# A search for places moved from a gather loop into the preparation ahead of it, in a two-layer graph network

## The chip, the cores and the metric

The kernel runs on one core of one Trainium2 chip. The metric is the device time of one execution in microseconds (us). Seven executions of the kernel before took 7149.64 to 7173.16 us, with a median of 7166.39 us. The engines are named as in the profile: PE (matrix products), PEld (its weight loads), DVE (vector), ACT (activations and copies), POOL (here above all the issuer of indirect DMAs, that is of gathers) and SP (issuer of plain DMAs).

## The reference

A graph has 12,500 nodes of 128 features and 412,500 edges sorted by destination. Two layers run one after the other:

```python
h = relu(layernorm(x))
msg = where(edge_type == 0, h[src] @ W_data.T + b_data, h[src] @ W_control.T + b_control)
x = x + relu(segment_sum(msg, dst) + h @ W_self.T + b_self)          # layer 0
h = relu(layernorm(x))
g = tanh((h @ gate_w[:128])[dst] + (h @ gate_w[128:])[src] + gate_b)
e = (g + tanh(edge_weight mixed by two scalars)) * 0.5 * d[dst] * d[src]   # d = degree ** -0.5
x = x + segment_sum(h[src] * e, dst)                                  # layer 1
```

The change touches what comes ahead of layer 0's sum over edges, and that sum's loop.

## The kernel before, in words

Nodes are kept in 98 blocks of 128 (NB), edges in tiles of 128. The program is traced as one long sequence, and a scheduler in the framework orders each engine's queue when the kernel is built. It may move an instruction ahead of others that come earlier in the program when it expects it to be ready; instructions marked to be kept in program order (indirect DMAs, the products of the loop) stay in order among themselves. Each engine then runs its queue strictly in order, waiting on semaphores. Pools are opened and closed in a nested way, so that a pool opened later reuses the space of one that was closed, after its last user.

**Preparation.** `nodes()` (L289 to L334) goes over the nodes in 14 batches of 7 blocks. A batch loads x (`xb`), computes means and scales on DVE (L217, L218), the normalised h on ACT (L312), turns h and multiplies it with the three weight matrices on PE (L315, L319), adds the biases on DVE (`y`, L321) and stores two message rows per node in `table1` and the self term in `agg1`. It also keeps h in bf16 parts in `H`. `edges()` goes over the edges in 13 steps: it loads source, destination, type and weight, forms the row of `table1` that each edge needs, turns everything and stores it as `idx1_d` (rows), `dst_d` (destinations) and others, and for later edges stores a flat copy `flat_d`. At its end `windows()` (three steps) finds the lowest and highest destination of each chunk of 28 tiles (`BASE`, `more`) and leaves the lowest destination of each late tile in `tmin`. Two steps of `edges()` follow each batch of nodes.

**The two halves of layer 0's sum.** Edges to the first 56 blocks of nodes (67 chunks of 28 tiles, 1876 tiles in all) are gathered: for each group of 4 tiles (469 groups, `group`, L487), POOL issues four indirect DMAs (L482) that fetch 128 message rows each into one of 8 buffers `M`, DVE builds one-hot matrices `oh` (L493), and PE multiplies and accumulates in `acc` (L258 is the line of the helper `product`). The rows come from `IDX`, the destinations from `DL`: two large tiles in on-chip memory, loaded whole (L461, L462), with `BASE` subtracted from `DL` in one instruction (L464). Edges to the last 42 blocks are not gathered but done densely (`counts`, L698 on): a matrix `A` that counts edges between nodes is built from pairs of codes, `QI` and `CI` (L707 and L709 on DVE, the product `pa` on PE, the copy L712 on ACT), and multiplied with `H` (the product `z`). This is cut into 8264 steps.

**The search.** The codes `QI` and `CI` need to know where each of 2688 pairs of nodes has its edges. `places()`/`sought()` (L511 on) find that: 21 comparisons of all of `tmin` with a bound (`junk`, L537), 21 indirect DMAs for a line of `flat_d` (L547) each followed by a comparison (L550), some arithmetic on 128x21 tiles, 21 indirect DMAs `g` (L577) in 7 blocks of 3, each block followed by some 20 DVE instructions (L589 to L621), and 59 transposes (L648) copied by ACT into `QI`, `CI` and a third array for layer 1. The same generator also zeroes `agg3` (L519 to L523), forms the bounds of a fallback loop, and in 8 steps (L682 to L695) prepares arrays for layer 1.

**The loop of layer 0** (L762 to L796) goes over the groups. After each group it advances the search by two steps; at `lead` = 20 groups the rest of the search is emitted at once, and from then on the dense steps are spread evenly over the remaining groups:

```python
                if not found:
                    found = next(find, True) is True or next(find, True) is True
                    if not found and at < lead:
                        continue
                    if not found:
                        for _ in find:
                            pass
                        found = True
                while done * (groups - lead) < steps * (at - lead):
                    done += 1
                    next(dense, None)
```

At the chunk boundaries the loop loads the rows of `agg1` that the chunk adds to (`old`, L264) and stores the sum (L271), both on SP. After the loop comes a node stage, then layer 1, whose loop gathers in the same way but loads its indices chunk by chunk (`edges_of`, L944, one chunk ahead, three buffers), and a last addition.

Of the kernel before, what the change touches and what calls it, by code (L numbers as in the profile page):

```python
# [18 lines left out]
P = 128  # L19
# [17 lines left out]
def kernel(  # L37
# [235 lines left out]
    with ExitStack() as first:  # L273
# [12 lines left out]
        IDX = pool.tile([P, T1], I32, name="IDX")  # L286
        DL = pool.tile([P, T1], F32, name="DL")
        OK = pool.tile([P, 2], F32, name="OK")

# [89 lines left out]
        def edges():  # L379
            with tc.tile_pool(name="edges", bufs=2) as pool, \  # L380
                    tc.tile_pool(name="edges_t", bufs=2, space=PSUM) as ps_t:
                EC = 2
                for c0 in range(0, NCH, EC):
# [65 lines left out]
                    yield  # L449
            yield from windows()  # L450

        edge_steps = edges()
        for k, _ in enumerate(nodes()):
            for _ in range(2):
                next(edge_steps, None)
        for _ in edge_steps:
            pass

        psum = first.enter_context(tc.tile_pool(name="loop0_p", bufs=1, space=PSUM))
        late0 = first.enter_context(tc.tile_pool(name="late0", bufs=1))  # L460
        nc.sync.dma_start(IDX, idx1_d[:, :T1])  # L461
        nc.sync.dma_start(DL, dst_d[:, :T1])  # L462
        local = DL.rearrange("p (c t) -> p c t", t=C)
        nc.vector.tensor_tensor(local, local, BASE[:, :NC0, None].to_broadcast([P, NC0, C]),  # L464
                                op=ALU.subtract)
        QI = late0.tile([P, NPAIR], F16, name="QI")
        CI = late0.tile([P, NPAIR], F16, name="CI")
# [42 lines left out]
        def places():  # L510
            with tc.tile_pool(name="places", bufs=1) as pool:  # L511
                yield from sought(pool)

        def sought(pool):

            none = pool.tile([P, NBATCH, D], F32, name="none")
            nc.vector.memset(none, 0.0)
            for b0 in range(0, NB, NBATCH):
# [5 lines left out]
            V = pool.tile([P, NJ], F32, name="V")  # L524
            nc.gpsimd.iota(V, pattern=[[2 * P, NJ]], base=N1, channel_multiplier=2,
                           allow_small_or_imprecise_dtypes=True)
            before = pool.tile([P, NJ], F32, name="before")
            inside = pool.tile([P, NJ], F32, name="inside")
            tile_i = pool.tile([P, NJ], I32, name="tile_i")
            rows = pool.tile([P, NJ], I32, name="rows")  # L530
            tile_f = pool.tile([P, NJ], F32, name="tile_f")
            found = pool.tile([P, NJ], F32, name="found")
            found2 = pool.tile([P, NJ2], F32, name="found2")
            first = pool.tile([P, NJ], F32, name="first")
            junk = pool.tile([P, TD], BF16, name="junk")
            for j in range(NJ):
                nc.vector.tensor_scalar(junk, tmin, V[:, j:j + 1], 0.0, op0=ALU.is_lt, op1=ALU.add,  # L537
                                        accum_out=before[:, j:j + 1])
                if j % 4 == 3:
                    yield  # L540
            nc.vector.tensor_scalar(tile_f, before, -1.0, 0.0, op0=ALU.add, op1=ALU.max)
            nc.vector.tensor_scalar(before, tile_f, float(T1 - TF), None, op0=ALU.add)
            nc.vector.tensor_copy(tile_i, before)
            yield
            for j in range(NJ):
                line = pool.tile([P, 8, 3, 16], F32, name="line", bufs=3)
                tc.keep_in_program_order(nc.gpsimd.indirect_dma_start(  # L547
                    out=line.rearrange("p a k e -> p (a k e)"), out_offset=None, in_=flat_d,
                    in_offset=bass.IndirectOffsetOnAxis(ap=tile_i[:, j:j + 1], axis=0)))
                nc.vector.tensor_scalar(junk[:, :P].rearrange("p (a e) -> p a e", e=16),  # L550
                                        line[:, :, 0, :], V[:, j:j + 1], 0.0, op0=ALU.is_lt,
                                        op1=ALU.add, accum_out=inside[:, j:j + 1])
                if j % 3 == 2:
                    yield
            start = pool.tile([P, NJ], F32, name="start")
            nc.vector.scalar_tensor_tensor(start, tile_f, float(P), inside, op0=ALU.mult,
                                           op1=ALU.add)
            nc.vector.tensor_scalar(start, start, 1.0 / 16, None, op0=ALU.mult)
            start = floored(pool, start, [P, NJ], "start")
            nc.vector.tensor_scalar(before, start, float((T1 - TF) * 8), None,  # L560
                                    op0=ALU.add)
            nc.vector.tensor_copy(rows, before)

            nc.vector.tensor_scalar(first, start, 16.0, -float((T2 - T1) * P), op0=ALU.mult,
                                    op1=ALU.add)
            nc.vector.tensor_scalar(start, start, -float(L2 * P // 16), 0.0, op0=ALU.add,
                                    op1=ALU.max)
            nc.vector.tensor_copy(ROWS2, start)
            yield
            q = pool.tile([P, NJ, P], F16, name="q")  # L570
            c = pool.tile([P, NJ, P], F16, name="c")
            c1 = pool.tile([P, NJ2, P], F16, name="c1")
            JB = 3
            for j0 in range(0, NJ, JB):
                g = pool.tile([P, JB, 8, 3, 16], F32, name="g", bufs=2)
                for j in range(JB):
                    tc.keep_in_program_order(nc.gpsimd.indirect_dma_start(  # L577
                        out=g[:, j].rearrange("p a k e -> p (a k e)"), out_offset=None,
                        in_=flat_d.rearrange("t (a e) -> (t a) e", a=8),
                        in_offset=bass.IndirectOffsetOnAxis(ap=rows[:, j0 + j:j0 + j + 1],  # L580
                                                            axis=0)))
                yield
                shape = [P, JB, 8, 16]
                dl, key = g[:, :, :, 0, :], g[:, :, :, 1, :]

                def by16(a):
                    return a.rearrange("p j (a e) -> p j a e", e=16)

                nc.vector.tensor_tensor(dl, dl, V[:, j0:j0 + JB, None, None].to_broadcast(shape),  # L589
                                        op=ALU.subtract)  # L590
                m0 = pool.tile(shape, F32, name="m0")
                m1 = pool.tile(shape, F32, name="m1")
                nc.vector.tensor_scalar(m0, dl, 0.0, None, op0=ALU.is_equal)
                nc.vector.tensor_scalar(m1, dl, 1.0, None, op0=ALU.is_equal)
                nc.vector.tensor_add(m0, m0, m1)
                nc.vector.tensor_reduce(found[:, j0:j0 + JB], m0, AX.XY, ALU.add)
                col = pool.tile(shape, F32, name="col")
                nc.vector.tensor_scalar(col, key, 1.0 / P, None, op0=ALU.mult)
                col = floored(pool, col, shape, "col")
                nc.vector.scalar_tensor_tensor(by16(q[:, j0:j0 + JB, :]), col, -float(P), key,  # L600
                                               op0=ALU.mult, op1=ALU.add)
                cj = by16(c[:, j0:j0 + JB, :])
                nc.vector.scalar_tensor_tensor(cj, m1, float(2 * NB), col, op0=ALU.mult,
                                               op1=ALU.add)
                nc.vector.scalar_tensor_tensor(cj, cj, 1.0, m0, op0=ALU.add, op1=ALU.mult)
                r0 = max(0, J2 - j0)
                if r0 < JB:
                    js2 = slice(j0 + r0 - J2, j0 + JB - J2)
                    ty = pool.tile(shape, F32, name="ty")
                    for r in range(r0, JB):  # L610
                        nc.vector.tensor_scalar(ty[:, r],
                                                iotas[:, :P].rearrange("p (a e) -> p a e", e=16),
                                                first[:, j0 + r:j0 + r + 1], 0.0, op0=ALU.add,
                                                op1=ALU.is_ge)
                    nc.vector.tensor_mul(m0[:, r0:], m0[:, r0:], ty[:, r0:])
                    nc.vector.tensor_reduce(found2[:, js2], m0[:, r0:], AX.XY, ALU.add)
                    nc.vector.tensor_scalar(ty, col, float(NB), None, op0=ALU.is_ge)
                    nc.vector.scalar_tensor_tensor(ty, ty, -float(NB), col, op0=ALU.mult,
# [16 lines left out]
            for k, t in enumerate((T1, T2)):  # L635
                nc.vector.tensor_scalar(OK[:, k:k + 1], pt[:, k:k + 1], float(E - t * P), None,
                                        op0=ALU.is_equal)
# [657 lines left out]
```

## Time and profile before

| | |
|---|---|
| median of 7 executions | 7166.39 us |
| the profiled execution | 7154.53 us, span 7152.8 us |
| first gather of layer 0 issued by POOL | 252.73 us into the span |
| first instruction of the dense half | 504.8 us |
| last product of layer 0's loop ends | 3347.2 us |
| busy over the span | PE 78%, PEld 62%, DVE 67%, ACT 44%, POOL 55% |

The page of the profile lists each engine's busy time, then the span in 40 equal slices (one is 178.8 us) with a digit for the busy tenths of each; PEclk is the tensor clock that was granted. A table by stretches gives, for each stretch, its length and then busy us and (number of instructions) of PE, PEld, DVE, ACT and POOL, then the granted clock, the DMA engines' busy share and GB/s. Groups of instructions are listed as: line, engine, operation, out<-in, shapes, count | busy us, mean ns of one | idle time of the engine just before them, and what ended it. A list of waits says who waited for whom: total us, times, longest us.

### The profile page before, as it was taken

How to read it: one execution, taken by the hardware profiler on the slowest of the kernel's cores; microseconds unless marked ns; L12 is line 12 of the kernel's file. 1: busy time of each engine (PE TensorE's matmuls, PEld its weight loads, DVE VectorE, ACT ScalarE, POOL GpSimd, SP SyncE). 2: the span in 40 equal slices, each digit the busy share in tenths (PEclk: the TensorE clock that was granted, in tenths of full speed). 3: DMA queues.
4: the chain of work that ended last, by engine and by line, in shares of the span. 5: the costliest groups of instructions: out<-in, count | busy, mean ns of one | idle time of the engine just before them, and what ended most of it. 6: DMA issues, size and time to landing. Idle time of an engine off the chain costs nothing. (4 is left out here: it accounts for less than half of the span.)

```text
span 7152.8 us, 106835 instructions
## 1 busy us (share of the span) xinstructions
PE 5601.4 (78%) x33125; PEld 4413.8 (62%) x33126; DVE 4807.2 (67%) x16203; ACT 3179.1 (44%) x9128; POOL 3926.6 (55%) x4152
## 2 busy tenths in 40 slices
PE   5338898898889888886288785887888888888884
PEld 3226676676666666665033233787887878878774
DVE  6556665666666666666777776776777777777775
ACT  6214444444444444443322223555555555555551
POOL 2465665565566556552255555555555555555552
PEclk7659999999999999998589997898989988888897
DMA  6421121121122112113544552111111111111115
GB/s 193 138 83 46 47 49 44 46 49 45 45 48 49 45 47 49 45 46 87 154 129 136 134 135 76 46 47 44 48 46 47 47 46 46 46 46 46 47 47 144
DMA packets 455853, 493.50 MB, mean 69 GB/s; under 512 B 131482, under 2 KB 352238, under 8 KB 455282
## 3 DMA queue, kind: packets, MB, share of 16 engines
q0 software_dynamic: 131360, 274.09, 15.8%
q1 hardware_dynamic: 272672, 185.32, 9.2%
q10 hardware_dynamic: 51250, 27.19, 1.4%
q8 instruction: 271, 4.44, 0.2%
q14 instruction: 300, 2.46, 0.1%
HBM read 411.55 MB, written 74.70 MB: 68 GB/s over the span
## 5 line engine op out<-in xcount | busy, mean ns | idle before, releaser
L899 POOL DMA_INDIRECT M<-table,ix x2128 | 2018.9, 949 | 1509.4 <-issue 749.5
L482 POOL DMA_INDIRECT M<-table,IDX x1876 | 1787.5, 953 | 1179.1 <-issue 448.8
L258 PE MATMUL z<-H,A 128*128 128x385 bf16 x8232 | 1901.4, 333 | 24.3 <-PE pa L258 14.5
L712 ACT CAST A<-pa 128x392 bf16<-128x392 f32 x2688 | 1270.8, 487 | 1340.2 <-PE z L258 629.8
L258 PEld LDWEIGHTS <-A 128*128 128x128 bf16 x8232 | 1130.2, 138 | 767.4 <-issue 480.3
L707 DVE TENSOR_SCALAR oq<-piota,QI 128x128 bf16<-128x128 f16 x2688 | 748.9, 279 | 892.4 <-PE z L258 428.1
L258 PE MATMUL acc<-M,oh 128*128 128x128 f32 (+1 forms) x8008 | 1182.2, 292 | 176.0 <-DMA M<-table,IDX 117.5
L258 PEld LDWEIGHTS acc<-M,oh 128*128 128x128 f32 x8008 | 1089.4, 204 | 335.6 <-issue 130.8
L258 PE MATMUL z<-A,HS 128*128 128x128 f32 x6664 | 1030.9, 293 | 166.5 <-issue 144.4
L258 PE MATMUL pa<-oc,oq 128*128 128x392 bf16 x2688 | 894.0, 333 | 319.7 <-issue 223.0
L709 DVE TENSOR_SCALAR oc<-piota,CI 128x392 bf16<-128x392 f16 x2688 | 1111.8, 414 | 0.0
L258 PEld LDWEIGHTS z<-A,HS 128*128 128x128 f32 x6664 | 953.2, 205 | 199.0 <-issue 176.8
L258 PE MATMUL pa<-oc,oe 128*128 128x196 f32 x4352 | 937.0, 361 | 154.6 <-ACT oe L1084 71.0
L1094 ACT COPY A<-pa 128x392 f32<-128x392 f32 x1088 | 500.3, 484 | 1045.4 <-PE pa L258 444.1
L258 PEld LDWEIGHTS pa<-oc,oe 128*128 128x128 f32 x4352 | 793.9, 209 | 199.7 <-ACT oe L1084 86.1
L912 ACT ACTIVATE gate<-e,M 128x1 f32<-128x1 f32 x2128 | 511.4, 292 | 629.9 <-DVE only L905 280.8
L905 DVE SCALAR_TENSOR_TENSOR only<-piota,dl,pd 128x128 f32<-128x128 f32 x2128 | 738.5, 347 | 61.6 <-remote 25.3
L920 DVE TENSOR_SCALAR oh<-piota,dl,e 128x128 f32<-128x128 f32 x2128 | 725.6, 404 | 0.1
L1084 ACT ACTIVATE oe<-oq,eb 128x128 f32<-128x128 f32 x2176 | 683.4, 393 | 45.4 <-DVE oh L920 13.4
L1079 DVE TENSOR_TENSOR oc<-piota,cb 128x784 f32<-128x784 f32 x544 | 526.0, 967 | 44.4 <-remote 14.8
L1076 DVE TENSOR_TENSOR oq<-piota,qb 128x512 f32<-128x512 f32 x544 | 371.7, 683 | 100.0 <-ACT oe L1084 100.0
L258 PE MATMUL ev<-ms,which 98*8 98x512 f32 x552 | 308.5, 643 | 81.1 <-DVE ms L998 65.2
(262 smaller groups left out, 3349.1 us busy)
## 6 DMA issues: line engine op xcount, KB each, us to landing
qs<-src_q SPq DMA_DIRECT2D x138, 256.0 KB
bs<-src_b SPq DMA_DIRECT2D x138, 256.0 KB
M<-table,ix POOLq DMA_INDIRECT x2128
M<-table,IDX POOLq DMA_INDIRECT x1876
table<-y SPq DMA_DIRECT2D x14, 903.0 KB
xb<-in_x_dram SPq DMA_DIRECT2D x26, 448.0 KB
agg<-y ACTq DMA_DIRECT2D x14, 451.5 KB
ga<-agg SPq DMA_DIRECT2D x14, 451.5 KB
```

The source lines that it names most:

```text
L258: tc.keep_in_program_order(nc.tensor.matmul(*args, **how))
L482: tc.keep_in_program_order(nc.gpsimd.indirect_dma_start(out=M[:, s, :], out_offset=None, in_=table1, in_offset=bass.IndirectOffsetOnAxis(a ...
L707: nc.vector.tensor_scalar(oq, iota_q, QI[:, k:k + 1], None, op0=ALU.is_equal)
L709: nc.vector.tensor_scalar(oc, iota_c, CI[:, k:k + 1], None, op0=ALU.is_equal)
L712: nc.scalar.copy(A[:, i], pa)
L899: tc.keep_in_program_order(nc.gpsimd.indirect_dma_start(out=M[:, s, :], out_offset=None, in_=table2, in_offset=bass.IndirectOffsetOnAxis(a ...
L905: nc.vector.scalar_tensor_tensor(only, iota_1, dl[:, s:s + 1], pd, op0=ALU.is_equal, op1=ALU.mult, accum_out=e[:, s:s + 1])
L912: nc.scalar.activation(gate[:, s:s + 1], e[:, s:s + 1], AF.Tanh, bias=M[:, s, D:])
L920: nc.vector.tensor_scalar(oh[:, s, :], iota_1, dl[:, s:s + 1], e[:, s:s + 1], op0=ALU.is_equal, op1=ALU.mult)
L1079: nc.vector.tensor_tensor(oc, iota_c[:, None, :].to_broadcast([P, 4, NC1]), cb[:, us, None].to_broadcast([P, 4, NC1]), op=ALU.is_equal)
L1084: nc.scalar.activation(oe[:, k, :], oq[:, k, :], AF.Copy, scale=eb[:, 4 * u + k:4 * u + k + 1])
L1094: nc.scalar.copy(A[:, 4 * u + k:4 * u + k + 2, :], pa)
```

## The change

The search becomes part of a generator `searched()` that runs `edges()`, `windows()` and `places()` one after another; four of its steps, in place of two, follow each batch of nodes, and whatever is left is emitted after the thirteenth of the 14 batches. The transposes of the codes are issued block by block inside the search, into two PSUM buffers; the scaling by `OK`, which the copies after the transposes did, becomes two DVE instructions over the whole of `CI` and `C1`. The buffers `line` and `g` have one copy less each. What the generator did beside the search (zeroing `agg3`, bounds, the arrays for layer 1) stays in the loop as `afterwards()`, one step per group. `lead` goes, and the dense steps are spread over all 469 groups. `IDX` and `DL` go: each chunk's `ix` and `dl` (14 KB each) are loaded two chunks ahead into three buffers, and DVE subtracts `BASE` for each.

The diff, cut to its core:

```diff
-        IDX = pool.tile([P, T1], I32, name="IDX")
-        DL = pool.tile([P, T1], F32, name="DL")
         OK = pool.tile([P, 2], F32, name="OK")
+        QI = pool.tile([P, NPAIR], F16, name="QI")
+        CI = pool.tile([P, NPAIR], F16, name="CI")
...
-            yield from windows()
-
-        edge_steps = edges()
-        for k, _ in enumerate(nodes()):
-            for _ in range(2):
-                next(edge_steps, None)
-        for _ in edge_steps:
-            pass
-
-        nc.sync.dma_start(IDX, idx1_d[:, :T1])
-        nc.sync.dma_start(DL, dst_d[:, :T1])
-        local = DL.rearrange("p (c t) -> p c t", t=C)
-        nc.vector.tensor_tensor(local, local, BASE[:, :NC0, None].to_broadcast([P, NC0, C]),
-                                op=ALU.subtract)
...
         def places():
-            with tc.tile_pool(name="places", bufs=1) as pool:
-                yield from sought(pool)
+            with tc.tile_pool(name="places", bufs=1) as pool, \
+                    tc.tile_pool(name="places_p", bufs=1, space=PSUM) as psum:
+                yield from sought(pool, psum)
...
-                line = pool.tile([P, 8, 3, 16], F32, name="line", bufs=3)
+                line = pool.tile([P, 8, 3, 16], F32, name="line", bufs=2)
...
-            q = pool.tile([P, NJ, P], F16, name="q")
-            c = pool.tile([P, NJ, P], F16, name="c")
-            c1 = pool.tile([P, NJ2, P], F16, name="c1")
+            C1 = pool.tile([P, NJ2 * P], F16, name="C1")
+            identh = pool.tile([P, P], F16, name="identh")
+            nc.vector.tensor_copy(identh, ident)
+
+            def turned(a, to, j0):
+                w = a.shape[1]
+                pt = psum.tile([P, 512], F32, name="misc", bufs=2).bitcast(F16)
+                for j in range(w):
+                    nc.tensor.transpose(pt[:, j * P:(j + 1) * P], a[:, j, :], identh)
+                nc.scalar.copy(to[:, j0 * P:(j0 + w) * P], pt[:, :w * P])
+
             JB = 3
             for j0 in range(0, NJ, JB):
-                g = pool.tile([P, JB, 8, 3, 16], F32, name="g", bufs=2)
+                g = pool.tile([P, JB, 8, 3, 16], F32, name="g", bufs=1)
...
+                turned(q, QI, j0)
...
+                turned(c, CI, j0)
...
+                    turned(c1, C1, j0 + r0 - J2)
...
+            nc.vector.tensor_scalar(CI, CI, OK[:, 0:1], None, op0=ALU.mult)
+            nc.vector.tensor_scalar(C1, C1, OK[:, 1:2], None, op0=ALU.mult)
+            nc.sync.dma_start(qi_d, QI)
+            nc.sync.dma_start(ci_d, C1)
             yield
-            for a, to, held_to in ((q, QI, qi_d), (c, CI, None), (c1, None, ci_d)):
...
+        def searched():
+            yield from edges()
+            yield from windows()
+            yield from places()
+
+        search = searched()
+        for k, _ in enumerate(nodes()):
+            for _ in range(4):
+                next(search, None)
+            if k == NB // NBATCH - 2:
+                for _ in search:
+                    pass
...
-        find = places()
+        find = afterwards()
         dense = counts()
-        found = False
         groups = T1 // S
-        lead = 20
         steps = PPH + NHB * NB
         done = 0
+        def edges_of(c):
+            ix = pool.tile([P, C], I32, name="ix", bufs=3)
+            nc.sync.dma_start(ix, idx1_d[:, c * C:(c + 1) * C])
+            dl = pool.tile([P, C], F32, name="dl", bufs=3)
+            nc.sync.dma_start(dl, dst_d[:, c * C:(c + 1) * C])
+            nc.vector.tensor_scalar(dl, dl, BASE[:, c:c + 1], None, op0=ALU.subtract)
+            return ix, dl
+
         last = old = None
+        ready = {c: edges_of(c) for c in range(2)}
         for c in range(NC0):
+            if c + 2 < NC0:
+                ready[c + 2] = edges_of(c + 2)
+            ix, dl = ready.pop(c)
             acc = psum.tile([P, D + 1], F32, name="acc", bufs=2)
             for g in range(0, C, S):
                 t = c * C + g
-                group(acc, IDX[:, t:t + S], DL[:, t:t + S], t, g == 0, g + S >= C)
+                group(acc, ix[:, g:g + S], dl[:, g:g + S], t, g == 0, g + S >= C)
...
-                if not found:
-                    found = next(find, True) is True or next(find, True) is True
-                    if not found and at < lead:
-                        continue
-                    if not found:
-                        for _ in find:
-                            pass
-                        found = True
-                while done * (groups - lead) < steps * (at - lead):
+                while done * groups < steps * at:
                     done += 1
                     next(dense, None)
+                next(find, None)
```

## The prediction

> **What bounds the kernel now.** I read the 40 slices of the page first. They show layer 0's loop full on PE from the fourth slice on, and a hole ahead of it.
>
> ```profile
> span 7152.8 us, 106835 instructions
> ...
> PE   5338898898889888886288785887888888888884
> ...
> PEclk7659999999999999998589997898989988888897
> ```
>
> The reader is to see the 3 in slices 2 and 3 of PE, and granted clocks of 0.6 and 0.5 there, between a preparation at 5 and a loop at 8 or 9. A table by stretches then cuts the hole open. Its limits are those of the stages: first gather at 252.73 us, comparisons of the search until 304, its first DMAs until 359, its blocks until 443, transposes until 505, the dense half until 3347.
>
> ```profile
> 0.00:150.00 150.00, 82.36 (x263) 45.98 (x264) 102.05 (x339) 87.51 (x199) 35.94 (x61) 0.80 0.74 206
> 150.00:252.00 102.00, 63.24 (x190) 33.92 (x190) 58.48 (x162) 58.85 (x140) 26.73 (x27) 0.83 0.46 131
> 252.00:304.00 52.00, 11.43 (x32) 7.80 (x32) 39.64 (x64) 0.00 (x0) 15.97 (x17) 0.50 0.55 159
> 304.00:359.00 55.00, 12.37 (x32) 8.01 (x32) 20.24 (x90) 0.00 (x0) 35.53 (x37) 0.50 0.42 122
> 359.00:443.00 84.00, 23.39 (x66) 15.50 (x67) 64.22 (x173) 3.14 (x7) 66.41 (x58) 0.50 0.39 113
> 443.00:505.00 62.00, 16.66 (x100) 15.09 (x99) 6.69 (x34) 8.27 (x9) 42.30 (x45) 0.53 0.26 70
> 505.00:3347.00 2842.00, 2500.69 (x15428) 1917.06 (x15428) 1803.43 (x5972) 1327.77 (x3023) 1668.13 (x1764) 0.97 0.19 46
> ```
>
> In the 253 us from 252 to 505 PE is busy for 64 us at half clock, in the 2842 us after it for 88%. In the same 253 us only 168 records of `acc` products stand, 8 for a group, so 21 groups of 469. Who sets the pace of the dense stage is told by the waits from 600 to 3300 us:
>
> ```profile
> POOL M L482 <- issue: 402.9, 1314, 0.6
> DVE oq L707 <- PE pa L258: 349.8, 269, 4.6
> POOL M L482 <- PE z L258: 309.0, 212, 6.0
> POOL M L482 <- PE pa L258: 221.5, 136, 7.6
> ```
>
> POOL, DVE and ACT wait for PE. The rate agrees: 632 `acc` records in each 500 us are 79 groups, 6.33 us a group, where POOL needs 4 x (0.95 + 0.30) = 5.0 us for its four gathers. So PE sets the end of this stage, and the 253 us before it are a wait for the search: the dense half cannot start without `QI` and `CI`.
>
> **The change, part by part.** Times are against the profiled execution (7154.53 us, 11.86 us under the median); the difference is then put on the median.
>
> *The hole goes.* Dense work no longer waits for 20 groups of gathers and the search. That takes away 505.4 - 252.7 = 252.7 us, and gives back three things.
>
> *The 21 groups* now run inside the dense stage. At the end of the loop, at full clock, a group's eight records start at 3304.78 and the next product at 3305.67: 0.89 us. 21 x 0.89 = 19 us. Their DVE and POOL parts lie beside PE: POOL's 5.0 us against a new pace of (2842 + 19) / 469 = 6.10 us.
>
> *The start of the dense half.* The first product needs four gathers (5.0 us) and a landing, some 3 us: 8 us behind the first gather. What stays in `afterwards()` (8 steps of some 2.6 us for layer 1's arrays, 6 us of bounds) falls on ten groups in which DVE is at 63% already: 26 us into some 60 us with 22 free. I give 8 us for it and for the 6.4 MB of zeroes beside the first gathers; both stood in the hole before. Nothing to 20 us.
>
> *The preparation grows.* This is the large unknown. DVE is the busiest engine there: 102.05 + 58.48 = 160.5 us, less `DL` and four `oh` that go or were the loop's, 155 us. The search's own DVE time: the four stretches from 252 to 505 hold 39.6 + 20.2 + 64.2 + 6.7 = 131 us, of which about 40 belong to `oh` (18 x 0.69), layer 1's arrays (20), bounds and the rest. That leaves 91 us. The two multiplications by `OK` are not in the trace; nearest is L709, 414 ns for 392 columns, so 2688 and 2176 columns are at most 5.1 us, at least nothing (no gain: the copies they relieve are ACT's). Sum 155 + 91 + 5 = 251 us.
>
> ```profile
> L537 DVE TENSOR_SCALAR_CACHE_REDUCE junk<-tmin,V 128x1347 bf16<-128x1347 f32 x21 | 33.9, 1614 | 5.1 <-POOL V L525 4.9
> L577 POOL DMA_INDIRECT g<-flat_d,rows x21 | 20.8, 991 | 10.8 <-issue 5.5 <-DVE start_f L566 4.7 <-DMA M<-table,IDX 0.6
> ```
>
> The other engines have room: POOL 63 us and 42 x 1.25 = 52 more; ACT 146, with 20 copies of 384 columns in place of nine of up to 896; PE 146, with the same 59 transposes. The bounds for the first gather: below, DVE never idle but for its first 8 us and the landing of the last table, 251 + 16 = 267 us. Above, the search simply put behind the old preparation: comparisons 45.5 us, 21 lines at 1.25 us and landings 32, to the first `g` 3, seven blocks 82, the end 5, together 168, so 421 us. That lower bound has reasons to fail: each comparison after a gather waits in DVE's queue for its landing, with the batch's arithmetic behind it; one buffer of `g` puts a block's three gathers behind the reads of the one before; POOL's subtractions for `H` and the search's gathers block each other in order. DVE's best long stretch in this very work, 359 to 443, was 76% busy. I take that: 251 / 0.76 = 330 us. So +77 us.
>
> *Indices by chunk.* `IDX` and `DL` go (issued at 112 and 123 us, hidden); 134 loads of 14 KB come, on SP. SP has idle time but waits in order: it stood 888 us for `o` of the dense half (longest 36.2) and 354 for `R` (longest 52.0). Behind a blocked load stand `old` and the next stores; POOL would wait for `ix`. The loads are two chunks (some 85 us) ahead, POOL runs at most 8 groups (49 us) ahead of PE; the margin is about 36 us less one landing. Layer 1 does the same one chunk ahead; POOL's idle time there names no load of `ix`:
>
> ```profile
>   issue: 749.5, 1726
>   ACT A L1094: 359.7, 156
>   ACT gate L912: 185.1, 69
> ```
>
> 67 subtractions at 236 ns (layer 1's L1148) are 16 us of DVE beside PE, with over 1000 us free. So I cost it at nothing. Uncovered, it costs a landing per chunk: the weights issued at 15.02 us were used at 18.26, 3.2 us x 67 = 214 us.
>
> [...]
>
> *Sum.* First gather 330, + 8 + 2842 + 19 + 8 = 3207 us in place of 3347: -140 us. Layer 1 is untouched. 7154.5 - 140 = 7014.5 for the profiled execution, 7166.4 - 140 = **7026 us** against the median.
>
> **Rivals.**
> *The search hides wholly in DVE's idle time* (92 of 252 us idle speaks for it, the waits in order against): first gather 267, -203 us, 6963.
> *The search is merely put behind the nodes*: for it, the chain of landings, one buffer of `g` and POOL in order; against it, the steps alternate with batches, which have idle DVE. First gather 421, -49 us, 7117. This is also the case where the move does not do what it says.
> *The loop is paced by groups, not by PE*: then 21 groups cost 21 x 6.33 = 133, not 19; -26 us, 7140. Against it: POOL waits for PE.
> *Slower: the chunk loads come late on SP*, held behind a store that waits for ACT's `o`, as the 36.2 and 52.0 us above allow. It decides from 140 / 67 = 2.1 us a chunk; at 3.2 us it is 214 - 140 = +74 us, 7240.
>
> **How the numbers follow.** Forecast 0.58, hidden wholly 0.18, put behind 0.12, paced by groups 0.05, late loads 0.07. The range goes from 6970 (near the full hiding) to 7120 (just past the search put behind), and leaves out the last two cases and the edges of the others, 0.2. A measurement here tells some 0.2% (14 us) from no change. Slower by more: 0.06 of the late loads. Within: 0.03, from the last two. Faster: 0.91.
>
> **What would show it.** The first gather at 300 to 370 us with DVE about 76% busy before it; the first `pa` about 8 us later; then 2860 to 2880 us to the end of the loop, 6.1 us a group, POOL still waiting for PE and not for `ix`; layer 1's length as before. I am wrong if the first gather comes after 421, if POOL or DVE wait for DMAs of `ix` or `dl`, or if the dense stage is longer than 2900 us.

## The result, and the profile after

The changed kernel takes 7210.29 us (median of 17 executions, 7195.93 to 7242.81), the kernel before beside it 7166.46 us (42 executions): a ratio of 1.0068, 95% interval [1.0057, 1.0078]. It is slower by 0.7% where 2% faster was forecast. The same kernel later gave 1.0008 [0.9984, 1.0032] beside other executions of the kernel before, so its cost lies between nothing and 0.7%; no run shows the forecast gain. The profiled execution took 7229.64 us, with a span of 7227.8 us.

Executions fell on chips of two speeds. The median of the kernel before is 7158 to 7188 us on some (three chips, "the slower chips" below) and 5791 to 5793 us on others (two, "the faster chips"). In the experiments a ratio is always to the kernel before on the same chip. The kernel after itself ran on slower chips alone.

The slices of the page answer to those of before:

```profile
span 7227.8 us, 107419 instructions
...
PE   5378888888888888887188885888888888878884
...
PEclk7689999999999999998589897998998899988897
```

Of the hole's two digits 3 on PE, one is left. But the loop behind it, which the forecast took for full, has no 9 where before had three, and it fills more of the 19th slice (7 in place of 6), not less. The stretches, cut at the first gather and the first dense product (us, then busy us and number of PE, PEld, DVE, ACT and POOL, granted clock, DMA share, GB/s):

```profile
0.00:314.00 314.00, 161.74 (x485) 84.26 (x486) 225.74 (x674) 148.40 (x348) 98.36 (x124) 0.72 0.58 161
314.00:375.00 61.00, 6.26 (x35) 4.09 (x36) 30.52 (x77) 6.02 (x13) 37.83 (x38) 0.50 0.31 95
375.00:3400.00 3025.00, 2583.93 (x15579) 1957.91 (x15578) 1861.90 (x6146) 1331.01 (x3020) 1739.80 (x1844) 0.95 0.20 49
```

The dense half starts at 375.4 us in place of 505.4, 130 us earlier. Its stage then lasts 3025 us in place of 2838: 187 us more, for 20 more groups. The loop's last gathered product is at 3395.1 us in place of 3338.1, +57; the other 18 us of the span's +75 lie behind the loop, where nothing was changed. (The 2838 us end with the last `z`, at 3343.8; the 2842 us of the prediction, and the 3347.2 us of the table ahead of it, run on to the closing products of the dense half.) In the stage PE is busy for 2583.93 of 3025 us: 441 us idle, where before had 340:

```profile
505.00:3343.00 2838.00, 2498.08 (x15415) 1915.64 (x15415) 1802.87 (x5971) 1327.20 (x3020) 1668.13 (x1764) 0.97 0.19 46
```

Who waits in that stage (600 to 3300 us; total us, times, longest us):

```profile
ACT A L712 <- PE z L258: 669.0, 583, 3.3
PEld L258 <- issue: 555.0, 782, 4.3
...
PE pa L258 <- issue: 274.6, 311, 4.1
...
DVE dl L772 <- DMA dl<-dst_d: 1.7, 2, 1.4
```

The last line clears the chunk loads: 1.7 us in all. The first three look like a circle: ACT waits for PE, and PE's weight loads and `pa` wait for nothing that the profile shows ("issue"; 467.0 and 218.4 us before). The timeline shows one turn of it (start us, us, engine, line, operation, and the idle time before with its releaser):

```profile
1507.26 1.05 PE L258 MATMUL acc<-M,oh 128*128 128x129 f32 x8
...
1509.14 0.66 PE L258 MATMUL z<-H,A 128*128 128x385 bf16 x3
...
1509.69 0.94 POOL L620 DMA_INDIRECT M<-table,ix  x1 [0.59 <-PE pa L258]
1510.20 0.49 ACT L712 CAST A<-pa 128x392 bf16<-128x392 f32 x1 [2.59 <-PE z L258]
1510.21 0.28 DVE L707 TENSOR_SCALAR oq<-piota,QI 128x128 bf16<-128x128 f16 x1 [2.14 <-PE z L258]
...
1510.74 0.33 PE L258 MATMUL pa<-oc,oq 128*128 128x392 bf16 x1 [0.94 <-issue]
```

The reader is to see the order. A group's eight gathered products stand at 1507.26. Some 2 us behind them POOL, ACT and DVE, idle until then, are released within 0.5 us of each other, all three by PE, though the `pa` that ACT copies ended 1.6 us before by its record (the line of 1508.31, 0.33 us long, is left out here). PE then stands 0.94 us because ACT and DVE were late. Such gaps of PE (over 0.4 us) come to 0.90 us a group, 0.71 before.

The trace also holds the times at which semaphores rise, and POOL, ACT and DVE wait here for one that PE raises at the ends of its products. In the kernel before, in the 252 us ahead of its first gather, it rises 0.01 us behind the end of each of the 266 products that raise it. In this turn of the kernel after it rises at 1510.18, 1.5 us behind the recorded end of `pa`, and ACT starts 0.02 us later. From 600 to 3300 us the next rise comes 0.21 us behind the end of such a product at the median, over 1.0 us behind one in ten, and 3.9 us behind at most. 881 times two rises stand 35 to 50 ns apart, where the recorded ends of two products that raise it are never less than 0.16 us apart. There it is PE's signals that are late, not its products.

### The profile page after: what moved, and what is told of

Read it like the earlier page. It is cut to its first block, busy times and chain, and to the rows that moved or that the text cites. A ratio compares the mean times of both kernels' runs of the same rounds, so it can differ in the third digit from the quotient of the medians.

```text
span 7227.8 us, 107419 instructions
## 1 busy us (share of the span) xinstructions
PE 5646.8 (78%) x33125; PEld 4411.4 (61%) x33126; DVE 4832.3 (67%) x16271; ACT 3175.5 (44%) x9135; POOL 3903.7 (54%) x4152
## 5 line engine op out<-in xcount | busy, mean ns | idle before, releaser
L902 POOL DMA_INDIRECT M<-table,ix x2128 | 2011.1, 945 | 1533.7 <-issue 742.3
L620 POOL DMA_INDIRECT M<-table,ix x1876 | 1772.0, 945 | 1276.5 <-issue 452.1
L258 PE MATMUL z<-H,A 128*128 128x385 bf16 x8232 | 1931.7, 337 | 28.1 <-PE pa L258 18.6
L1001 DVE SCALAR_TENSOR_TENSOR ms<-bs,pidx,gp 98x512 f32<-98x512 f16 x276 | 203.3, 745 | 254.3 <-PE gp L258 74.8
```

Of the source, the lines that this page charges most:

```text
L258: tc.keep_in_program_order(nc.tensor.matmul(*args, **how))
L620: tc.keep_in_program_order(nc.gpsimd.indirect_dma_start(out=M[:, s, :], out_offset=None, in_=table1, in_offset=bass.IndirectOffsetOnAxis(a ...
L902: tc.keep_in_program_order(nc.gpsimd.indirect_dma_start(out=M[:, s, :], out_offset=None, in_=table2, in_offset=bass.IndirectOffsetOnAxis(a ...
```

## Experiments

The first account was: the dense stage has become dearer. Either *by its loads* (indices by chunk, on SP and DVE), or *by its groups* (each costs some 6 us there, whatever stands beside it, and the hole had hidden 20 of them).

**Indices whole again, and the dense half's place.** `e1_whole_idx` is the kernel after with `IDX` and `DL` whole and `afterwards()` emitted ahead of the loop:

```diff
+        nc.sync.dma_start(IDX, idx1_d[:, :T1])
+        nc.sync.dma_start(DL, dst_d[:, :T1])
...
-            ix, dl = ready.pop(c)
+            ix, dl = IDX[:, c * C:(c + 1) * C], DL[:, c * C:(c + 1) * C]
```

> The changed kernel with IDX and DL loaded whole again, ahead of the loop, and with everything of afterwards() emitted ahead of the loop (the two large tiles leave no room for it beside the dense half), which starts the dense half some 30 us later. Theory C, the chunk loads: each of the 67 chunk boundaries stalls the loop by some 2 us, through DVE's subtraction or SP; then the dense stage, 3027 us in the changed kernel, falls to 2860 to 2890 us, and the time to about 7100 us. Theory S, the spreading: the dense stage grows because 469 groups, not 448, interrupt it and because 17.6 steps in place of 18.4 fall between two groups, which leaves PE at half clock more often; then the stage stays at 3000 to 3030 us and the time is about 7230 us.

`e2_chunks` is the kernel before with the loads by chunk (the opposite edit):

> The kernel before with one part of the change: ix and dl loaded by chunk, two chunks ahead, in place of IDX and DL. Theory C: the dense stage grows from 2842 us to about 2970, the time from 7166 to about 7295 us. Theory S: the dense stage stays within 20 us of 2842, the time within 20 us of 7166.

`e3_lead` is the kernel after with the dense half held back for 20 groups, as before:

```diff
-                while done * groups < steps * at:
+                while done * (groups - 20) < steps * (at - 20):
```

> The changed kernel with the dense steps spread over the last 449 groups again, as before the change; the first 20 groups run alone, at POOL's 5 us a group, beside the end of the search. Theory S: the dense stage is 2842 us within 20 and starts at about 420 us, so it ends near 3262, and the time is about 7075 us. Theory C: the stage is about 2970 us and the time about 7200 us.

`e4_whole_lead` has both edits, with `afterwards()` left in the loop:

> Both undone: IDX and DL whole, dense steps over the last 449 groups; what is left of the change is the search in the preparation. Both theories: dense stage 2842 us within 20, start at about 420 us, time about 7075 us. If the stage is longer than 2900 us, both are wrong, and something that the move itself does to the order of the queues is the cause.

Measured: e1 1.0040 [1.0016, 1.0064], e2 0.9974 [0.9951, 0.9998], e3 0.9936 [0.9894, 0.9978], e4 0.9968 [0.9946, 0.9990]. The loads are no cost: alone they change the time by -0.3%, and taken out of the changed kernel they leave its long stage (e1: 3057 us). The stage's length goes with the number of groups in it: 2838 to 2906 us where it has 448 (before, e2, e3, e4), 3025 to 3057 us where it has 468 (after, e1). Theory C falls with e1 and e2. Theory S's own numbers for e3 and e4 (7075 us) were missed: they took 7135 and 7155 us, since the dense half started at 502 and 495 us and not at 420, and the stages were over 50 us longer than 2842. Holding the dense half back for 20 groups, that is giving most of the gained start away again, made the kernel no slower.

**What the gathers cost, part by part.** `e5_dense_only` leaves the gathered half out, `e6_no_gather` leaves only the 1876 indirect DMAs out (`held` is a buffer of constants, given to every group of layer 0):

```diff
-            M = pool.tile([P, S, D + 1], F32, name="M", bufs=MB)
-            for s in range(w):
-                gather(M, s, ix[:, s:s + 1])
+            if held is None:
+                M = pool.tile([P, S, D + 1], F32, name="M", bufs=MB)
+                for s in range(w):
+                    gather(M, s, ix[:, s:s + 1])
+            else:
+                M = held
```

> The changed kernel with the gather half of layer 0's loop left out (no gathers, one-hots, products, loads and stores of its 469 groups): what the 8264 dense steps cost by themselves. If a group costs what PE's records show (0.89 us), the stage is some 2884 - 469 x 0.89 = 2470 us at full clock. If the loop is paced by its groups, each of which costs 5 us or so, it is far shorter, about 1900 us, near the sum of the dense records (8232 x 0.165 + 2688 x 0.165 + 84 x 2.3 = 1995 us).

> The changed kernel with the 1876 indirect DMAs left out: the products of every group run as they did, on one buffer of constants. If it is the gathers (POOL's pace, their traffic) that make a group dear, the stage falls to the dense one alone plus 469 x 0.89 = 417 us. If it is the products on PE, or the interruption of the chain PE, ACT, DVE by them, it stays near 3025 us, or 2884 us less half-clock time.

`e7_spread_400` is the kernel after with the dense steps spread over the first 400 groups only, so that 20.7 of them stand beside a group in place of 17.7:

```diff
-                while done * groups < steps * at:
+                while done < steps and done * 400 < steps * at:
```

> The changed kernel with the dense steps spread over the first 400 groups, 20.7 steps a group, and the last 69 groups by themselves at POOL's 5 us. Theory S in its strict form (a group in the dense stage costs 5 us or more, whatever steps stand beside it): the dense half ends after some 400 x 6.2 = 2480 us at full clock, 2600 with half-clock time, and 69 x 5 = 345 us follow, so that the time is some 80 us below the changed kernel's. If a group costs 0.89 us, the dense half takes 2884 - 69 x 0.89 = 2823 us and the 345 us come on top: some 280 us above it.

`e8_before_again` is the kernel before, for a profile of the same chip:

> The kernel before, profiled a second time on the chip of these runs. All theories: the dense stage is 2842 us long within 30. How far it and its half-clock time (151 us in the first profile) differ tells how much of the differences between the stages of two profiles is chance.

These four fell on a faster chip, where the kernel before takes 5790.93 us. They gave 5288.7 us (e5), 5721.63 (e6), 5986.67 (e7, 1.0338 [1.0321, 1.0355]) and 5793.47 (e8). There the dense stage is what the forecast took it for. The stretch of the dense stage in e8, the kernel before:

```profile
465.00:2840.00 2375.00, 2369.58 (x15416) 1889.04 (x15416) 1832.24 (x5969) 1371.89 (x3020) 1690.09 (x1787) 1.00 0.26 56
```

PE is busy for 2369.58 of 2375 us, at a clock of 1.00. And there a tighter spread costs 3.4%: it lengthens the tail of gathers at the end of the loop (310 us in e7), in which PE has little to do (197 us busy). Whether the move pays on such a chip was not run; an estimate from e7's start of the dense half (372.7 us) and e6's stage (2412 us) ends it at 2785 us, 55 us before e8's.

So the same kernels were run on a slower chip, with the kernel after beside them:

> The changed kernel without the gather half of layer 0's loop, again, since the last four kernels ran on a chip on which the kernel before takes 5791 us and its dense stage stands without gaps. On a chip where it takes 7166 us: if the gaps in front of pa come with the groups' products, they vanish here and the stage is near 1995 us; if the chain of PE, ACT and DVE stalls by itself on such a chip, the stage is 2300 us or more.

> The changed kernel without the 1876 indirect DMAs, again. On a chip where the kernel before takes 7166 us: if the gathers cause the gaps, the stage is 2412 us as on the other chip; if the products do, it stays near 3025 us.

> The changed kernel with the dense steps over the first 400 groups, again. On a chip where the kernel before takes 7166 us and 1.0 to 1.4 us is lost in each group of the dense stage: the dense half ends after 2348 + 416 x 1.2 = 2850 us, the last groups add 5 us each, 260 us, and the time is some 60 us above the changed kernel's. If the loss belongs to steps, not groups, the dense half takes 2900 us or more.

> The changed kernel beside the kernel before, on the chip of these runs. Where the kernel before takes 5791 us (dense stage 2375 us, no gaps) the working of the prediction should hold: dense start near 375 instead of 465 us, stage 2375 + 18 us, so 70 us faster, 5720 us. Where it takes 7166 us, 40 to 50 us slower, with a stage near 3025 us.

Measured: f5 6092.27 us, f6 6509.69, f7 6965.61 (0.9749 [0.9722, 0.9776]), f9 7164.16 (1.0008 [0.9984, 1.0032]). Between f5 and f6 lie 417 us for 469 groups of products: 0.89 us a group, the very term of the prediction. The stage of f6, with all products and no indirect DMA:

```profile
364.00:2775.00 2411.00, 2396.71 (x15577) 1906.31 (x15575) 1865.56 (x6145) 1372.63 (x3020) 0.00 (x0) 0.99 0.04 10
```

2411 us for 468 groups, 5.15 a group, PE full: this is what PE needs, on the slower chips as on the faster (2412 in e6). The same products behind gathers take 3025 us. So the gathers cost the stage 614 us, and f7 says that the cost shrinks when more dense steps stand beside each group: on the slower chips the tighter spread that loses 3.4% on the faster gains 2.5%. That was not expected: f7 was forecast some 60 us above the kernel after, and f9 itself 40 to 50 us above the kernel before.

**Issue or transfer, floor or price, move or spread.** `g1_spread_430` is f7 with 430 in place of 400:

> The kernel after with the dense steps spread over the first 430 groups (19.2 steps a group in place of 17.6); 39 groups of gathers are left behind for PE to do without dense work. Theory G (a group beside dense work costs about 6.2 us whatever number of steps stands beside it): the stage of dense work has some 440 groups and lasts about 440 x 6.2 = 2730 us, the rest of the gathers adds some 39 x 5 = 195 us, and the loop ends near 3310, between the kernel after (3395) and the spread over 400 (3223). Rival P (PE paces the stage: 8264 steps cost the same, spread as they like): the stage is as long as the kernel after's, 3027, less only 0.89 us for each of the 28 groups it is rid of, and the tail is added: slower than the kernel after by some 100 us.

`g2_before_spread` puts the same spread on the kernel before:

```diff
-                while done * (groups - lead) < steps * (at - lead):
+                while done < steps and done * (400 - lead) < steps * (at - lead):
```

> The kernel BEFORE (search still in layer 0's loop) with the dense steps spread over groups 21 to 400 in place of 21 to 469. It tells whether the gain of the spread over 400 (ratio 0.975 on the kernel after) is the spread's alone or needs the move. Theory M (where PE is kept full, the move pays what was forecast): it is slower than the kernel after with the same spread, by 252.7 us of hole less 77 us of longer preparation less 19 us for 21 groups and some 35 us of late start: some 100 to 120 us. Rival S (the move gives nothing in any spread, since its 21 groups cost what the hole cost): both take the same time within 30 us.

`g4_spread_400` is f7 once more, beside it:

> The kernel after with the dense steps spread over the first 400 groups, once more, beside the same spread on the kernel before. Expected as the last time: loop's end near 3223, ratio about 0.975 to the kernel before. Theory M has it some 100 to 120 us faster than the kernel before with the same spread, rival S within 30 us of it.

`g3_plain_loads` keeps the transfers and takes them from POOL (`plain` is set in layer 0's loop):

```diff
-                gather(M, s, ix[:, s:s + 1])
+                if plain:
+                    r = (t + s) * P
+                    nc.sync.dma_start(M[:, s, :], table1[r % (NB * P):r % (NB * P) + P, :])
+                else:
+                    gather(M, s, ix[:, s:s + 1])
```

> The kernel after with each of layer 0's 1876 gathers replaced by a plain load of 128 consecutive rows of the same table into the same buffer, issued by SP; the sums of layer 0 over the gathered edges are therefore those of other rows. Same products, same bytes, same number of transfers; POOL issues no indirect DMA in this loop. Theory D (the gathers' making on POOL, their descriptors, is what delays PE's signals and costs half clock): stage near that without gathers, 2411 us for 468 groups, without gaps. Rival B (the transfers themselves, bytes into memory beside PE, cost the gaps): stage near the kernel after's, 3027 to 3036 us, with gaps of some 1.1 us a group.

Measured: g1 7100.52 us, 0.9897 [0.9861, 0.9934]; g2 6966.63, 0.9713 [0.9677, 0.9748]; g4 6986.06, 0.9738 [0.9701, 0.9775]; g3 6520.13. The stage of g3:

```profile
363.00:2775.00 2412.00, 2393.77 (x15578) 1902.40 (x15577) 1866.23 (x6145) 1369.84 (x3020) 0.00 (x0) 1.00 0.26 61
```

As many bytes land in the same buffers (DMA share 0.26, more than the 0.20 of the kernel after), and the stage is as short as without any. In f6 and g3 PE's semaphore rises 0.01 us behind the end of a product, 99 times in 100. So it is not the amount of traffic that makes 2412 us into 3025, but that POOL issues it as indirect DMAs; the rival that blames the bytes falls. One difference g3 leaves: its rows are consecutive, those of the gathers scattered. Against it stands that the gathers land as soon on both kinds of chips (the last packet of one comes 1.22 us behind the end of POOL's instruction in the kernel after, 1.28 us in e7; medians, packets taken in order).

The profiled runs of layer 0 with groups on the slower chips, by the dense steps beside one group (rounded down to whole us). "PE's need" is f6's 2411 us less 0.89 us for each group that the stage lacks. It is good to some 20 us: for the 448 groups of the kernel before it gives 2393 us, and e8 took 2375. Half clock is the time in the stage at half the tensor clock, at which eight gathered products took 2.06 us (at 373.58 us in the kernel after), for 1.05 us at full (at 1507.26 us); the last column is the stage less half of that time, for each group.

| kernel | steps a group | groups | stage, us | PE's need | excess | half clock, us | us a group |
|---|---|---|---|---|---|---|---|
| after, f9, e1 | 17.7 | 468 | 3025, 3036, 3057 | 2411 | 614 to 646 | 287, 280, 341 | 6.16 to 6.19 |
| before, e2, e3, e4 | 18.4 | 448 | 2838, 2893, 2906, 2896 | 2393 | 445 to 513 | 151, 235, 245, 214 | 6.17 to 6.23 |
| g1 | 19.3 | 429 | 2777 | 2376 | 401 | 184 | 6.26 |
| g4, f7 | 20.7 | 399 | 2499, 2480 | 2350 | 149, 130 | 65, 37 | 6.18, 6.17 |
| g2 | 21.8 | 379 | 2350 | 2332 | 18 | 26 | 6.17 |
| f6, g3 (no indirect DMA) | 17.7 | 468 | 2411, 2412 | 2411 | 0, 1 | 29, 21 | 5.12, 5.13 |

With four gathers, every row gives 6.2 to 6.3 us a group, whatever number of steps stands beside it. At 21.8 steps PE's own need is 2332 / 379 = 6.15 us a group, as long as that pace, and the excess is nearly gone. So in these runs on the slower chips a group of four gathers has a floor of about 6.2 us beside dense work (6.16 to 6.26 in the table); PE's need shows only above it. A price on each gather does not fit: at 614 / 468 = 1.31 us a group, 523 us would be left in g4, where 149 were measured. Rival P of g1, in which PE paces the stage, falls. Theory G holds, though the stage of g1 has 429 groups and not the 440 of its forecast, and the loop ended at 3350 us, not 3310.

And the move? g2, without it, is no slower than g4, with it (6966.63 and 6986.06 us, overlapping intervals); theory M asked for 100 to 120 us between them. The stretches from the first dense product to its end and of the tail, g2 first, then g4:

```profile
505.00:2855.00 2350.00, 2326.18 (x14866) 1825.03 (x14866) 1773.24 (x5892) 1341.35 (x3020) 1428.95 (x1515) 0.99 0.22 48
2855.00:3210.00 355.00, 119.66 (x551) 101.06 (x550) 46.09 (x76) 0.16 (x1) 233.93 (x248) 0.57 0.23 50
```

```profile
384.00:2883.00 2499.00, 2389.37 (x15024) 1846.42 (x15023) 1802.46 (x6060) 1338.73 (x3020) 1510.65 (x1596) 0.99 0.24 52
2883.00:3241.00 358.00, 119.47 (x555) 102.17 (x554) 47.34 (x83) 0.16 (x1) 234.57 (x248) 0.57 0.23 50
```

The dense half starts 121 us earlier in g4 and lasts 149 us longer: 20 groups at the pace of the table are 123 us, half of the added half-clock time is 20. Both beat both kernels of this study, by the spread alone.

The tails speak of the same thing. With no dense work beside them, the last 69 groups take 358 us in g4, 5.2 us each, while PE works for 119 us and POOL for 235. On the faster chip the same tail takes 310 us (e7), which is what 248 gathers every 1.25 us need. Three lines of g4's tail (lines of POOL and SP between them left out):

```profile
2993.05 2.09 PE L258 MATMUL acc<-M,oh 128*128 128x129 f32 x8 [5.85 <-issue]
...
3007.69 0.69 DVE L631 TENSOR_TENSOR oh<-piota,dl 128x512 f32<-128x512 f32 x1 [14.70 <-remote]
...
3008.43 2.09 PE L258 MATMUL acc<-M,oh 128*128 128x129 f32 x8 [13.30 <-issue]
```

PE's products end at 2995.1 by the records; DVE's next `oh` comes 12.5 us later, having waited 14.70 us for something that the profile can't name ("remote"), while POOL issued a gather every 1.25 us throughout. The record of the semaphores can: `oh` waits for the one that PE raises. Behind these products it rose at 2995.76, 2997.87 and 3007.66, and DVE started 0.02 us after the last of these. At 3020.27, with POOL idle since 3015.0, it rose ten times in 0.38 us, where eight products took 2.09 us: signals that had been held back, not products that ended then. In e7's tail every rise stands 0.01 us behind the end of its product. PE goes on 0.05 us after DVE's end. It is the way from PE's products to those who wait for them that is late, not the way back.

**Two that told little.** Two last kernels were to split the cause further. `g6_half_plain` replaces every second gather by a plain load, `g5_unread` lets the gathers run and the products read a constant buffer:

> The kernel after with every second gather of layer 0 replaced by a plain load of 128 consecutive rows, issued by SP (so half of the gathered edges get other rows). Theory F (a floor: a group of four gathers by POOL takes some 6.1 us, and PE's own need of 5.15 us shows only above it): with two gathers the floor is near 3.1 us, the stage is PE's own, about 2411 us, without gaps. Rival A (each indirect DMA adds its price, 614 us / 1872 = 0.33 us): half of it stays, about 2720 us.

> The kernel after with its gathers issued and landing as before, but layer 0's products over the gathered edges read a constant buffer, so PE does not wait for a landing and POOL does not wait for PE; those sums are therefore of constants. Theory I (issuing alone delays the signals by which PE releases ACT and DVE): gaps of 0.5 us a group or more remain, the stage of 468 groups lasts 2700 us or more. Rival W (the cost needs the wait of POOL for PE and of PE for the gather): no gaps, stage near that without gathers, 2411 us, POOL done early.

Both fell on a faster chip (kernel before 5792.7 us), which has no excess to split: g6's stage of 2412 us (5726.05 in all) is PE's need, but full gathers leave it there too. g5 took 7051.05 us, for another reason. From 600 to 2700 us (the second line is from the list of SP's own queue):

```profile
DVE dl L774 <- DMA dl<-dst_d: 1197.6, 23, 72.2
```

```profile
SPq L771 <- DMA M<-table,ix: 1831.7, 147, 34.5
```

With POOL free to run ahead, SP's load of the next `ix` waits for the gathers that still read its buffer (1831.7 us), the load of `dl` stands behind it on SP, DVE waits for that in order (1197.6 us), and PE waits for DVE (`pa` for `oc`, 1125.1 us). That is a late load, as in the prediction's slower rival, but held by the gathers' reads of `ix` and not by a store. In the kernel after it does not happen (1.7 us of waits); there POOL runs at most the 8 buffers `M` ahead.

## Why the prediction was wrong

**The step that failed** is "*The 21 groups* now run inside the dense stage ... 21 x 0.89 = 19 us", with its ground, "So PE sets the end of this stage". The 0.89 us are right (f5 against f6), and on the faster chips PE does set the end (busy for 2369.58 of 2375 us in e8). On the slower chips the 20 groups cost 187 us: about 123 by the pace (20 x 6.16) and 68 by half the added half-clock time, (287 - 151) / 2. The stage passed the 2900 us that the prediction gave as a sign of being wrong. Of the 198 us by which the dense half's closing products ended later than forecast (3405 us for 3207), 161 are this stage and 37 its later start. The kernel before already ran at this pace, 445 us above PE's need, and so the hole was not idle time to be won: its 21 groups went through there beside the search, at no cost to the dense stage. The trace had shown it. PE was busy for 2500.69 of 2842 us at a clock of 0.97, so 341 us were missing, and the waits from 600 to 3300 us held a line that I passed over:

```profile
PEld L258 <- issue: 467.0, 669, 4.0
```

That POOL waits for PE did not say here that PE is busy; PE's word came late (in this stretch 0.27 us behind the end of a product at the median, over 1.0 us behind one in ten).

**The start of the dense half**, forecast 8 us behind the first gather, came 61 us behind it. The first gather at 314.6 us (forecast 330) was near, but for another reason than given: it waits (5.23 us) for the last store of `table1` by the nodes, not for the end of the search. The search's last lines stand here:

```profile
356.79 0.56 DVE L531 TENSOR_TENSOR g<-g,V 128x384 f32<-128x384 f32 x1 [12.33 <-DMA g<-flat_d,rows]
...
371.15 0.78 DVE L587 TENSOR_SCALAR C<-C,OK 128x2176 f16<-128x2176 f16 x1
...
373.58 2.06 PE L258 MATMUL acc<-M,oh 128*128 128x129 f32 x8 [3.57 <-DVE oh L631]
```

The last block's `g` stood in POOL's queue behind the first gathers of the loop; DVE waited 12.33 us for its landing, and the loop's `oh` and products stand in order behind the block's arithmetic. The dense half began 37 us later than forecast (375.4 for 338).

**What was right.** DVE's work in the preparation: forecast 251 us, measured 225.74 + 30.52 = 256 up to 375 us; but DVE was busy for 68% of it, not 76. The two multiplications: 0.92 + 0.78 us, within their bound of 5.1. The loads by chunk, nothing: 1.7 us of waits, and 0.9974 [0.9951, 0.9998] alone. The 8 us for `afterwards()` could not be told apart in the stage.

**The rivals.** The one that came nearest was "paced by groups" (7140 us, at 0.05): its mechanism is the one shown, but it left out the later start and the half clock. Late loads, the slower rival, did not happen. "Hidden wholly" and "put behind the nodes" asked about the preparation, which lay between them and was not what decided.

**Open.** Why PE's signals come late while POOL issues indirect DMAs, and why on some chips only. What sets the floor at 6.2 us, where POOL's own four gathers need 5.0 us: the last two runs did not reach a chip that shows it, and the floor is read from the table alone.

## What to carry to other kernels

An engine that everyone waits for is the bound only where it is busy: compare its busy time at the granted clock with the stage, and if a tenth is missing (here 341 of 2842 us), find what it waits for before pricing moved work at that engine's rate. Work that runs in a hole may be getting a price there that it has nowhere else; run the loop without one of its parts (here without the gathers) before counting on the hole. An even spread is not neutral either: on the slower chips a spread over 400 of 469 groups gave 2.5 to 2.9%, with or without the move, and on a faster one it cost 3.4% (on the kernel after).

## What the runs showed of the hardware

- One kernel, two kinds of chips: the kernel before takes 7166 and 5791 us. Its dense stage lasts 2838 and 2375 us, and what lies behind that stage in the profiled executions (before and e8) 3810 and 2952 us, while POOL's gathers take 946 ns each on both.
- On the slower chips the signals by which PE releases others came late while POOL issued indirect DMAs. In the kernel before they rose 0.01 us behind the end of each of 266 products ahead of its first gather, and in its dense stage (600 to 3300 us) 0.27 us behind at the median and over 1.0 us behind one in ten. In the turn of the kernel after shown above it was 1.5 us, in g4's tail 12.5 us; in f6, in g3 and, on a faster chip, in e8 it was 0.01 us (medians). As many bytes as plain loads by SP did not cost the stage what the indirect DMAs did (2412 us in g3, 3025 in the kernel after). ACT waits as DVE does, and in the turn above both are released together by PE (1510.20 and 1510.21 us). DVE's own work keeps its length (`oc` takes 414 ns in the kernels before and after, 412 in e8), and a gather's first packet comes 0.70 us behind the end of POOL's instruction in the kernel after as in e7 (medians).
- Gaps of PE cost twice, as time and as clock: with 0.71 us of gaps a group the stage stood 151 us at half clock (before), with 0.90 us 287 us (after), without gaps 21 to 29 us (g3, f6). In the traces of the kernels before and after all changes of the granted clock (335 and 391) stand whole multiples of 3.413 us apart. PE was not idle through the whole step ahead of a fall: in the dense stage of the kernel before it had been busy for 0.37 to 1.59 us of the 3.41 us ahead of each of 28 falls, and for 1.54 us or more in each of the 759 other such steps at full clock.
